# Norms by narrow matmuls of tokens and squares, with other matmul budgets per tick, in a hybrid scan, attention and experts kernel

## The chip, the cores and the metric

The kernel runs on one core of one Trainium2 chip. The metric is device time in microseconds (us) of one execution; the figure quoted for a kernel is the median of its runs. Besides the timed runs there is one profiled execution, from which all durations of single instructions come.

## The reference, cut to what matters

Four images of 384 channels and 32 x 32 places (1024 tokens) go through two layers. Layer 0 is a group norm, a selective scan in four directions with 16 states, a norm over channels, a GELU, and a residual sum. Layer 1 is a norm over channels, causal attention with one head of width 384, a residual sum, another norm over channels, and a mixture of 4 experts of which each token takes 2, with a residual sum.

```python
x = x + _L0_conv_ref(_gn(x), ...)          # scan; then norm over channels, GELU
t = _to_tokens(x)
t = t + _L1_attn_ref(_ln_t(t), Wq, Wk, Wv)
t = t + _L1_ffn_ref(_ln_t(t), gate_w, gate_b, w1, b1, w2, b2)

def _layernorm(x, axis=-1, eps=1e-5):
    m = jnp.mean(x, axis=axis, keepdims=True)
    v = jnp.var(x, axis=axis, keepdims=True)
    return (x - m) / jnp.sqrt(v + eps)
```

All of it is in float32. The norms that the change touches are the one after the scan (its result goes through the GELU) and the one ahead of the experts. The attention's own norm is another function and isn't edited.

## The kernel before, in words

**Layout.** Channels lie on the 128 partitions, three blocks of 128 (`M` = 3) beside each other; tokens lie along the free axis. A sum over channels is therefore a matmul with a matrix of 1/384 (`mean_w`).

**Ticks.** The kernel is one hand-written order, produced by a loop over ticks (the loop at the end of `hybrid_kernel`). There are 768 units of scan (4 images x 3 blocks x 4 directions x 4 groups of states x 4 groups of channels), one a tick; image b has ticks 192b to 192b + 191. In a tick, ScalarE makes the decay of the unit two ticks on (L554), VectorE makes the input product `v` (`front`, L561) and the scan (`middle`, L567), GpSimd multiplies the scan before by its output weights (`back`, L584), and each fourth tick TensorE sums four units into `y` (`row`, L609). In ticks 0 to 191 part of the products `v` is made on TensorE instead (`feed`, `turned`, L872). `ahead` makes VectorE wait, ahead of `v`, for the decay of its unit and, each fourth tick, for `y` of the four units before.

**Everything else is a generator that runs beside the scan.** A generator yields `("pe", n)` when it has issued matmuls that it declares at n us, `("wait", n)` to sleep n ticks, and `("inner", 0)` to go on in the next tick ahead of the scan rather than after it. In a tick the order is: decays, work that was deferred (`due`), `ahead`, `v`, `back`, deferred inner work, parked generators (`unpark`), the scan, `row`, fetches of the scan's operands (SP queue), one step of the preparation of a coming image (`preparation`, `project_dt`), and then `go_on`. `go_on` adds the pace to an allowance of TensorE time, lets every side generator issue until it has spent its own budget of 1.0 (it may overdraw), takes that from the allowance, and gives what is left to the first waiting generator, `behind(b)`: attention of image b, then its experts. The pace is `PACE_A` = 4.4 in attention and `PACE_E` = 3.3 otherwise. Side generators are `finish(b)` (block norm, GELU and residual of image b), `ready(b, h)` (expert norm and gates of half h), `fold` (once) and loads. After tick 767 there is no scan, and the loop goes on until all is issued.

**Image b after its scan.** `evict` (L629) adds the skip term to `y`; for the last block of channels it starts `finish(b)` and queues `behind(b)`. `behind` waits until `finish` has added the residual (L893), then runs `attention` and `experts`. Attention's scores use one folded matrix in place of Wq and Wk: `fold` centres and turns Wq and Wk (L746), multiplies them (L757) and centres Wv (L769), once, at tick 192, and stores both results to DRAM (`g_d`, `wv_d`); every image reads them from there.

**The norm before the change** (`layernorm(dst, src, name, lag)`, L636 to L712; `finish` calls it with 1024 tokens and lag 0, `ready` with 512 and lag 1):

1. For each half of 512 tokens, the mean over channels, on all 128 output partitions, by 3 full matmuls (L652); 2.6 is declared for each.
2. VectorE subtracts it from the tokens (L660).
3. ScalarE squares the result (L672).
4. Four matmuls side by side in four column groups of 32 give the variance of 128 tokens each, 12 for a half (L679).
5. ScalarE takes the root (L687), VectorE the reciprocal (L692).
6. TensorE spreads the reciprocals to all partitions (L698), and VectorE multiplies (L708).

**Shared buffers.** PSUM banks for all this are two before tick 192 and four after (`banks`); 8 tiles in SBUF are shared as `slots` (squares, `xr`, `dt`, `du`, expert weights, attention weights and so on). What is given back comes free a tick later for slots and at once for banks; a generator that finds none sleeps a tick. The buffers `a0` (1) and `ht` (2) are larger ones, used by fold, attention and experts.

Of the kernel before, what the change touches and what calls it, by code (L numbers as in the profile page):

```python
# [8 lines left out]
F32 = mybir.dt.float32  # L9
AF = mybir.ActivationFunctionType  # L10
ALU = mybir.AluOpType
# [4 lines left out]
P = 128  # L16
B = 4
C = 384
M = C // P
HW = 32  # L20
L = HW * HW
# [21 lines left out]
AHEAD = 5  # L43
SLOTS = 8
PACE_A = 4.4
PACE_E = 3.3


@with_exitstack
def hybrid_kernel(  # L50
# [22 lines left out]
    nc = tc.nc  # L73
# [4 lines left out]
    one = ctx.enter_context(tc.tile_pool(name="one", bufs=1))  # L78
# [34 lines left out]
    inner = {}  # L113
# [4 lines left out]
    class Shared:  # L118
# [520 lines left out]
    def layernorm(dst, src, name, lag):  # L639

        width = src.shape[2]
        n = width // 512
        mus = []
        for h in range(n):
            mu = yield from banks.take(f"mu_{name}_{h}")  # L650
            for c in range(M):
                nc.tensor.matmul(  # L652
                    mu, mean_w, src[:, c, bass.ts(h, 512)], start=(c == 0), stop=(c == M - 1)
                )
            mus.append(mu)
            yield "pe", 2.6
        yield "inner", 0
        for h in range(n):
            s = bass.ts(h, 512)
            nc.vector.tensor_tensor(  # L660
                dst[:, :, s], src[:, :, s], mus[h].unsqueeze(1).to_broadcast([P, M, 512]),
                ALU.subtract,
            )
            banks.give(f"mu_{name}_{h}")
        sqs = []
        for c in range(M):
            sq = yield from slots.take(f"sq_{name}_{c}", P, width)
# [22 lines left out]
        banks.give(f"var_{name}")  # L690
        yield "wait", 1
        nc.vector.reciprocal(rs, rs)  # L692
        yield "wait", lag
        backs = []
        for h in range(n):
            spread_ = yield from banks.take(f"rb_{name}_{h}")
            for q in range(4):
                nc.tensor.matmul(  # L698
                    spread_[:, q * P : (q + 1) * P],
                    ident[:, 32 * q : 32 * q + 1].to_broadcast([P, P]), rs[:, h, :],  # L700
                    start=True, stop=True,
                )
# [12 lines left out]

    def fold():

        extra = pools["a0"].tile([P, M, L], F32, tag="a0", name="w_extra")
        extra = extra.rearrange("p m l -> p (m l)")
        vs = extra[:, : 2 * M * C].rearrange("p (j c d) -> p j c d", j=2, c=M)
        centre = extra[:, 2 * M * C : 2 * M * C + 2 * P].rearrange("p (j d) -> p j d", j=2)
        nc.sync.dma_start(vs[:, 0], wv.rearrange("(c p) d -> p c d", p=P))
        for same in range(2):
            nc.vector.scalar_tensor_tensor(
                centre[:, same, :], ident, float(same), mean_w, ALU.mult, ALU.subtract
            )  # L730
        def square(name):
            t = pools["ht"].tile([P, M, L], F32, tag="ht", name=name)
            t = t.rearrange("p m l -> p (m l)")[:, : 2 * M * C]
            return t.rearrange("p (j c d) -> p j c d", j=2, c=M)

        raw = square("w_raw")
        for j, w in enumerate((wq, wk)):
            nc.sync.dma_start(raw[:, j], w.rearrange("(c p) d -> p c d", p=P))
        wt = square("w_t")
        yield "wait", 2  # L740
        for j in range(2):
            for d in range(M):
                ps = yield from banks.take(f"pwt_{j}_{d}")
                for c in range(M):
                    for o in range(M):
                        nc.tensor.matmul(  # L746
                            ps[:, c * P : (c + 1) * P], raw[:, j, o, d * P : (d + 1) * P],
                            centre[:, int(o == c), :], start=(o == 0), stop=(o == M - 1),
                        )
# [604 lines left out]
    def step(g, budget):  # L1354

        if g in ended:
            ended.remove(g)
            return None
        while budget > 0 and until.get(id(g), -100) <= clock[0]:
            try:  # L1360
                what, n = next(g)
            except StopIteration:
                return None
            if what == "pe":
                budget -= n
            elif what == "inner":
                parked.append(g)
                until[id(g)] = clock[0] + 1
            elif what == "start":
                started.append(1)  # L1370
                break
            elif n > 0:
                until[id(g)] = clock[0] + n
        return budget

    def go_on():
        spare[0] = min(spare[0] + pace[0], pace[0])
        for g in side[:]:
            left = step(g, 1.0)
            if left is None:  # L1380
                side.remove(g)
            else:
                spare[0] -= 1.0 - left
        while waiting and spare[0] > 0:
            left = step(waiting[0], spare[0])
            if left is None:
                waiting.pop(0)
                continue
            spare[0] = left
            break  # L1390
# [13 lines left out]
    t = 0  # L1404
# [86 lines left out]
```

## Time and profile before

| | |
|---|---|
| Median of 3 runs | 3749.89 us (3745.99 to 3752.34) |
| Profiled execution | 3747.14 us |
| Its span, first to last instruction | 3745.0 us |
| Busy: TensorE matmul | 3350.6 us (89%) |
| Busy: VectorE | 2961.6 us (79%) |
| Busy: ScalarE | 2085.8 us (56%) |
| Busy: GpSimd | 1817.8 us (49%) |
| Mean granted TensorE clock | 0.932 |

How to read the profile's lines. A group's line has the line of the kernel, the engine, the operation, what is written and read, and the size (partitions x elements). A wait's line has who waited, for whom, the sum in us, how often, and the longest. A line of the timeline has start, length, engine, line, operation and how many instructions were merged into it; in brackets is the idle time before it and what ended it. A line of a table by stretch has the stretch, its length, the busy time and number of instructions of TensorE, weight loads, VectorE, ScalarE and GpSimd, the granted clock, the busy share of DMA and GB/s. Each float32 matmul of the program is two records in the trace. A busy TensorE is not TensorE at its peak, since its records overlap.

### The profile page before, as it was taken

The numbers are of one execution on the slowest core, as the hardware profiler recorded it, in microseconds if no ns is written. First come the engines' busy times: TensorE is split into PE (matmuls) and PEld (weight loads), VectorE is DVE, ScalarE is ACT, GpSimd is POOL, SyncE is SP. The second block draws the span as 40 slices with busy tenths as digits, with TensorE's granted clock in tenths as the row PEclk, the third lists the DMA queues.
The fourth block names the chain that finished last, engine by engine and source line by source line (L and its number), as shares of the span: only waits on it lengthen the run. The fifth ranks groups of instructions, "written<-read, shape, count | busy, mean of one in ns | idle before, by whom it ended". The sixth has DMA issues, their size and how long they took to land. (4 is left out here: it accounts for less than half of the span.)

```text
span 3745.0 us, 35189 instructions
## 1 busy us (share of the span) xinstructions
PE 3350.6 (89%) x11891; PEld 1529.0 (41%) x11891; DVE 2961.6 (79%) x2084; ACT 2085.8 (56%) x2832; POOL 1817.8 (49%) x776
## 2 busy tenths in 40 slices
PE   4666667789999999898999999889999998999999
PEld 1333333345333343344333344454344444544444
DVE  5999899988998998989998999999999982210000
ACT  4788888556666555566655555455554552412121
POOL 2777777555565565545555665455665650000000
PEclk7677777899999999999999999899999999999999
DMA  6665666645665756436666665455657551322321
GB/s 204 219 233 199 208 218 221 215 145 199 235 222 201 260 206 230 155 138 228 217 221 229 201 210 192 146 182 188 223 192 240 179 182 38 92 82 83 96 82 53
DMA packets 408019, 680.03 MB, mean 182 GB/s; under 512 B 33520, under 2 KB 279968, under 8 KB 407840
## 3 DMA queue, kind: packets, MB, share of 16 engines
q1 hardware_dynamic: 401632, 677.40, 53.0%
q8 instruction: 94, 1.54, 0.2%
q10 hardware_dynamic: 6208, 0.39, 0.1%
q14 instruction: 85, 0.70, 0.1%
HBM read 605.16 MB, written 72.55 MB: 181 GB/s over the span
## 5 line engine op out<-in xcount | busy, mean ns | idle before, releaser
L584 POOL TENSOR_TENSOR h<-h,bc 128x1024 f32<-128x1024 f32 x768 | 1816.7, 2370 | 1264.9 <-DVE v L561 1058.3
L567 DVE TENSOR_TENSOR_SCAN h<-da,v 128x1024 f32<-128x1024 f32 x768 | 1748.4, 2283 | 48.4 <-PE v L872 17.3
L554 ACT ACTIVATE da<-dt,a 128x1024 f32<-128x1024 f32 x768 | 886.5, 1162 | 868.1 <-DVE h L567 759.3
L1297 PE MATMUL fy<-ht,w 128*128 128x512 f32 x2304 | 1019.8, 599 | 7.5 <-ACT ht L1261 5.9
L1272 PE MATMUL ph<-fx,w 128*128 128x512 f32 x2304 | 1019.1, 598 | 3.8 <-DMA w<-in_w 2.9
L561 DVE TENSOR_TENSOR v<-du,bc 128x1024 f32<-128x1024 f32 x664 | 842.8, 1269 | 61.9 <-DMA du<-dts 25.9
L1297 PEld LDWEIGHTS fy<-ht,w 128*128 128x128 f32 x2304 | 435.6, 191 | 580.3 <-issue 551.0
L1272 PEld LDWEIGHTS ph<-fx,w 128*128 128x128 f32 x2304 | 433.4, 191 | 579.6 <-issue 529.5
L609 PE MATMUL y<-h,sel 128*32 128x512 f32 x3072 | 493.3, 657 | 91.2 <-POOL h L584 89.2
L1257 ACT ACTIVATE ht<-ph,b1s 128x512 f32<-128x512 f32 x384 | 257.9, 679 | 471.0 <-PE ph L1272 469.2
L1306 DVE SCALAR_TENSOR_TENSOR fy<-fy,b2s,tw 128x512 f32<-128x512 f32 x96 | 72.0, 750 | 423.0 <-PE fy L1297 423.0
L609 PEld LDWEIGHTS y<-h,sel 128*32 128x32 f32 x3072 | 96.6, 115 | 399.3 <-issue 220.3
L850 ACT ACTIVATE st<-turn,bt 128x128 f32<-128x128 f32 x832 | 244.2, 554 | 0.0
L872 PE MATMUL v<-ident,st 128*128 128x128 f32 x832 | 147.5, 337 | 86.2 <-DVE h L567 85.4
L1261 ACT ACTIVATE ht<-ht 128x3072 f32<-128x3072 f32 x64 | 176.9, 2764 | 0.8
L872 PEld LDWEIGHTS v<-ident,st 128*128 128x128 f32 x832 | 121.7, 175 | 127.7 <-DVE h L567 74.2
L554 ACT ACT_TABLE_LOAD x99 | 127.0, 1283 | 18.7 <-DMA dt<-dts 12.3
L425 PE MATMUL pdt<-xd,wdt 12*128 12x512 f32 x184 | 88.0, 813 | 45.7 <-ACT dt L433 22.6
L1079 PE MATMUL po<-pt,vt 128*128 128x256 f32 x480 | 102.8, 364 | 7.1 <-ACT pt L971 7.1
L1009 PE MATMUL ss<-axn,qt 128*128 128x512 f32 (+3 forms) x288 | 102.3, 503 | 3.9 <-ACT yb L1096 3.9
L1079 PEld LDWEIGHTS po<-pt,vt 128*128 128x128 f32 x480 | 90.4, 192 | 22.3 <-ACT pt L971 10.1
L1009 PEld LDWEIGHTS ss<-axn,qt 128*128 128x128 f32 x288 | 51.5, 196 | 47.1 <-issue 33.5
(208 smaller groups left out, 1612.3 us busy)
## 6 DMA issues: line engine op xcount, KB each, us to landing
bc<-rows SPq DMA_DIRECT2D x384, 512.0 KB, 4.7
w<-in_w SPq DMA_DIRECT2D x384, 384.0 KB, 6.0
dt<-dts SPq DMA_DIRECT2D x192, 512.0 KB, 4.5
du<-dts SPq DMA_DIRECT2D x192, 512.0 KB, 6.6
dts<-dt SPq DMA_DIRECT2D x48, 512.0 KB, 4.7
dts<-du SPq DMA_DIRECT2D x48, 512.0 KB, 5.3
fx<-t2d SPq DMA_DIRECT2D x12, 768.0 KB, 5.5
tw<-mkd SPq DMA_DIRECT2D x32, 256.0 KB, 6.2
```

The source lines that it names most:

```text
L554: u["decay"] = nc.scalar.activation(u["da"], spread["dt4", n], AF.Exp, scale=a4[:, g, u["q"] : u["q"] + 1])
L561: return nc.vector.tensor_tensor(u["v"], spread["du4", n], spread["bc", n][:, 0, :], ALU.mult)
L567: nc.vector.tensor_tensor_scan(u["h"][:, ::step], u["da"][:, ::step], u["v"][:, ::step], 0.0, op0=ALU.mult, op1=ALU.add,)
L584: product = units[n]["product"] = nc.gpsimd.tensor_tensor(h, h, spread["bc", n][:, 1, :], ALU.mult)
L609: units[n]["row"] = nc.tensor.matmul(y, sel, h, start=first, stop=last, tile_position=(0, jj * DJ))
L850: nc.scalar.activation(st[:, 4 * h + t, :].rearrange("p (d i) -> p i d", i=NI)[:, i, :], ps[h][:, t * P : (t + 1) * P], AF.Copy, scale=bt[ ...
L872: nc.tensor.transpose(u["v"][:, t * P : (t + 1) * P], st[:, t, u["j"] * P : (u["j"] + 1) * P], ident)
L1079: nc.tensor.matmul(pv[:, o:], vt[:, j, m * P : (m + 1) * P], pts[step][j // 4][:, j % 4, o:], start=(alone and j == 0), stop=(j == nj - 1),)
L1257: nc.scalar.activation(ht[:, f, :], ps, AF.Identity, bias=bias)
L1261: nc.scalar.activation(ht, ht, AF.Gelu)
L1272: nc.tensor.matmul(ps, tiles[n][:, c, (f % 2) * P : (f % 2 + 1) * P], xns[h][:, c, :], start=(c == 0), stop=(c == M - 1),)
L1297: nc.tensor.matmul(pss[m], tiles[n][:, f, :], hts[fh][:, f, :], start=(fh == 0 and f == 0), stop=(fh == 1 and f == FH - 1),)
```

## The change

- `layernorm` no longer subtracts first. It squares the tokens themselves, takes the means of tokens and of squares by matmuls in four column groups (12 each for a half), makes the variance as mean of squares less squared mean, and forms 1/root and mean/root on 128 x 256 elements (or 128 x 128). TensorE spreads both, and VectorE multiplies the tokens by the one and subtracts the other. The results are kept in the first tile of squares, no longer in a tile of their own. It declares 0.7 for each 12 matmuls of means and 1.8 for each half's spreading.
- Side generators may issue until they have spent `BESIDE` = 3.0 a tick instead of 1.0. `PACE_E` goes from 3.3 to 3.2.
- `fold` issues two banks' work a tick instead of one. Its Wv and its centring matrices move from the `a0` buffer to three slots, and it stores both results at the end.
- For image 0, `attention` makes the normed tokens before it waits for `fold` and loads the folded weights; for the other images the order stays.

```diff
@@ -43,7 +43,8 @@
 AHEAD = 5
 SLOTS = 8
 PACE_A = 4.4
-PACE_E = 3.3
+PACE_E = 3.2
+BESIDE = 3.0
 @with_exitstack
@@ -645,23 +646,6 @@
         width = src.shape[2]
         n = width // 512
-        mus = []
-        for h in range(n):
-            mu = yield from banks.take(f"mu_{name}_{h}")
-            for c in range(M):
-                nc.tensor.matmul(
-                    mu, mean_w, src[:, c, bass.ts(h, 512)], start=(c == 0), stop=(c == M - 1)
-                )
-            mus.append(mu)
-            yield "pe", 2.6
-        yield "inner", 0
-        for h in range(n):
-            s = bass.ts(h, 512)
-            nc.vector.tensor_tensor(
-                dst[:, :, s], src[:, :, s], mus[h].unsqueeze(1).to_broadcast([P, M, 512]),
-                ALU.subtract,
-            )
-            banks.give(f"mu_{name}_{h}")
         sqs = []
         for c in range(M):
             sq = yield from slots.take(f"sq_{name}_{c}", P, width)
@@ -669,47 +653,54 @@
         for h in range(n):
             for c in range(M):
                 s = bass.ts(h, 512)
-                nc.scalar.activation(sqs[c][:, s], dst[:, c, s], AF.Square)
+                nc.scalar.activation(sqs[c][:, s], src[:, c, s], AF.Square)
         yield "wait", lag
+
         var = yield from banks.take(f"var_{name}")
-        for h in range(n):
-            for c in range(M):
-                for q in range(4):
-                    o = h * 512 + q * P
-                    nc.tensor.matmul(
-                        var[32 * q : 32 * (q + 1), h * P : (h + 1) * P], mean_w[:, :32],
-                        sqs[c][:, o : o + P], start=(c == 0), stop=(c == M - 1),
-                        tile_position=(0, 32 * q),
-                    )
-            yield "pe", 1.0
-        slots.give(*[f"sq_{name}_{c}" for c in range(M)])
-        rs = one.tile([P, n, P], F32, tag=f"rs{n}", name=f"rs_{name}")
-        nc.scalar.activation(
-            rs, var[:, : n * P].rearrange("p (h t) -> p h t", t=P), AF.Sqrt, bias=eps
-        )
+        w = n * P
+        for o, of in ((w, [src[:, c, :] for c in range(M)]), (0, sqs)):
+            for h in range(n):
+                for c in range(M):
+                    for q in range(4):
+                        k = h * 512 + q * P
+                        nc.tensor.matmul(
+                            var[32 * q : 32 * (q + 1), o + h * P : o + (h + 1) * P],
+                            mean_w[:, :32], of[c][:, k : k + P],
+                            start=(c == 0), stop=(c == M - 1), tile_position=(0, 32 * q),
+                        )
+                yield "pe", 0.7
+        slots.give(*[f"sq_{name}_{c}" for c in range(1, M)])
+        rs = sqs[0][:, :w]
+        mean = sqs[0][:, w : 2 * w]
+        nc.scalar.activation(rs, var[:, w : 2 * w], AF.Square)
+        yield "inner", 0
+        nc.vector.tensor_tensor(rs, var[:, :w], rs, ALU.subtract)
+        nc.scalar.activation(rs, rs, AF.Sqrt, bias=eps)
+        yield "wait", 1
+        nc.vector.reciprocal(rs, rs)
+        nc.vector.tensor_tensor(mean, var[:, w : 2 * w], rs, ALU.mult)
         banks.give(f"var_{name}")
-        yield "wait", 1
-        nc.vector.reciprocal(rs, rs)
         yield "wait", lag
-        backs = []
-        for h in range(n):
-            spread_ = yield from banks.take(f"rb_{name}_{h}")
-            for q in range(4):
-                nc.tensor.matmul(
-                    spread_[:, q * P : (q + 1) * P],
-                    ident[:, 32 * q : 32 * q + 1].to_broadcast([P, P]), rs[:, h, :],
-                    start=True, stop=True,
-                )
-            backs.append(spread_)
-            yield "pe", 1.0
-        yield "inner", 0
         for h in range(n):
             s = bass.ts(h, 512)
-            nc.vector.tensor_tensor(
-                dst[:, :, s], dst[:, :, s], backs[h].unsqueeze(1).to_broadcast([P, M, 512]),
-                ALU.mult,
-            )
-            banks.give(f"rb_{name}_{h}")
+            while not banks.ready(2):
+                yield "wait", 1
+            both = [banks.now(f"{x}_{name}_{h}") for x in ("rb", "mb")]
+            for x, v in zip(both, (rs, mean)):
+                for q in range(4):
+                    nc.tensor.matmul(
+                        x[:, q * P : (q + 1) * P],
+                        ident[:, 32 * q : 32 * q + 1].to_broadcast([P, P]),
+                        v[:, h * P : (h + 1) * P], start=True, stop=True,
+                    )
+            yield "pe", 1.8
+            if h == n - 1:
+                slots.give(f"sq_{name}_0")
+            yield "inner", 0
+            x, y = (v.unsqueeze(1).to_broadcast([P, M, 512]) for v in both)
+            nc.vector.tensor_tensor(dst[:, :, s], src[:, :, s], x, ALU.mult)
+            nc.vector.tensor_tensor(dst[:, :, s], dst[:, :, s], y, ALU.subtract)
+            banks.give(*[f"{x}_{name}_{h}" for x in ("rb", "mb")])
     folded = []
@@ -719,62 +710,74 @@
-        extra = pools["a0"].tile([P, M, L], F32, tag="a0", name="w_extra")
-        extra = extra.rearrange("p m l -> p (m l)")
-        vs = extra[:, : 2 * M * C].rearrange("p (j c d) -> p j c d", j=2, c=M)
-        centre = extra[:, 2 * M * C : 2 * M * C + 2 * P].rearrange("p (j d) -> p j d", j=2)
-        nc.sync.dma_start(vs[:, 0], wv.rearrange("(c p) d -> p c d", p=P))
+        def square(name):
+            t = pools["ht"].tile([P, M, L], F32, tag="ht", name=name)
+            t = t.rearrange("p m l -> p (m l)")[:, : 2 * M * C]
+            return t.rearrange("p (j c d) -> p j c d", j=2, c=M)
+
+        raw = square("w_raw")
+        for j, w in enumerate((wq, wk)):
+            nc.sync.dma_start(raw[:, j], w.rearrange("(c p) d -> p c d", p=P))
+        va = yield from slots.take("va", P, 2, C)
+        vb = yield from slots.take("vb", P, C)
+        centre = yield from slots.take("centre", P, 2, P)
+        wvs = wv.rearrange("(c p) d -> p c d", p=P)
+        nc.sync.dma_start(va, wvs[:, :2, :])
+        nc.sync.dma_start(vb, wvs[:, 2, :])
+        vs = (va[:, 0, :], va[:, 1, :], vb)
         for same in range(2):
             nc.vector.scalar_tensor_tensor(
                 centre[:, same, :], ident, float(same), mean_w, ALU.mult, ALU.subtract
             )
-        def square(name):
-            t = pools["ht"].tile([P, M, L], F32, tag="ht", name=name)
-            t = t.rearrange("p m l -> p (m l)")[:, : 2 * M * C]
-            return t.rearrange("p (j c d) -> p j c d", j=2, c=M)
-
-        raw = square("w_raw")
-        for j, w in enumerate((wq, wk)):
-            nc.sync.dma_start(raw[:, j], w.rearrange("(c p) d -> p c d", p=P))
         wt = square("w_t")
-        yield "wait", 2
-        for j in range(2):
-            for d in range(M):
-                ps = yield from banks.take(f"pwt_{j}_{d}")
-                for c in range(M):
-                    for o in range(M):
-                        nc.tensor.matmul(
-                            ps[:, c * P : (c + 1) * P], raw[:, j, o, d * P : (d + 1) * P],
-                            centre[:, int(o == c), :], start=(o == 0), stop=(o == M - 1),
-                        )
-                yield "wait", 1
-                nc.scalar.copy(wt[:, j, d, :], ps[:, :C])
-                banks.give(f"pwt_{j}_{d}")
-        g = square("g_s")[:, 0]
-        for m in range(M):
-            ps = yield from banks.take(f"pg_{m}")
+
+        def turned_weight(j, d, ps):
+            for c in range(M):
+                for o in range(M):
+                    nc.tensor.matmul(
+                        ps[:, c * P : (c + 1) * P], raw[:, j, o, d * P : (d + 1) * P],
+                        centre[:, int(o == c), :], start=(o == 0), stop=(o == M - 1),
+                    )
+            return lambda: nc.scalar.copy(wt[:, j, d, :], ps[:, :C])
+
+        def product(m, ps):
             for d in range(M):
                 nc.tensor.matmul(
                     ps[:, :C], wt[:, 0, d, m * P : (m + 1) * P], wt[:, 1, d, :],
                     start=(d == 0), stop=(d == M - 1),
                 )
-            yield "wait", 1
-            nc.scalar.activation(g[:, m, :], ps[:, :C], AF.Copy, scale=-scale)
-            banks.give(f"pg_{m}")
-        yield "wait", 1
-        nc.sync.dma_start(g_d, g)
-        for m in range(M):
-            ps = yield from banks.take(f"pwv_{m}")
+            return lambda: nc.scalar.activation(both[:, 0, m, :], ps[:, :C], AF.Copy, scale=-scale)
+
+        def centred(m, ps):
             for c in range(M):
                 nc.tensor.matmul(
-                    ps[:, :C], centre[:, int(c == m), :], vs[:, 0, c, :],
+                    ps[:, :C], centre[:, int(c == m), :], vs[c],
                     start=(c == 0), stop=(c == M - 1),
                 )
-            yield "wait", 1
-            nc.scalar.copy(vs[:, 1, m, :], ps[:, :C])
-            banks.give(f"pwv_{m}")
-        yield "wait", 1
-        nc.sync.dma_start(wv_d, vs[:, 1])
+            return lambda: nc.scalar.copy(both[:, 1, m, :], ps[:, :C])
+
+        def by_twos(what, jobs):
+            for n in range(0, len(jobs), 2):
+                some = jobs[n : n + 2]
+                while not banks.ready(len(some)):
+                    yield "wait", 1
+                names = [f"{what}_{n + i}" for i in range(len(some))]
+                moves = [f(banks.now(name)) for f, name in zip(some, names)]
+                yield "wait", 1
+                for move in moves:
+                    move()
+                banks.give(*names)
+
+        yield "wait", 2
+        pairs = [(j, d) for d in range(M) for j in range(2)]
+        yield from by_twos("pwt", [lambda ps, j=j, d=d: turned_weight(j, d, ps) for j, d in pairs])
+        both = square("g_s")
+        jobs = [lambda ps, m=m: product(m, ps) for m in range(M)]
+        yield from by_twos("pg", jobs + [lambda ps, m=m: centred(m, ps) for m in range(M)])
+        slots.give("va", "vb", "centre")
+        nc.sync.dma_start(g_d, both[:, 0])
+        nc.sync.dma_start(wv_d, both[:, 1])
+        yield "wait", 1
         folded.append(1)
@@ -954,8 +957,10 @@
     def attention(b, yb, fx0):
         alone = b == B - 1
-        while not folded:
-            yield "wait", 1
+        if b == 0:
+            xn = yield from scaled_tokens(b, yb)
+            while not folded:
+                yield "wait", 1
         gw_ = []
         for name, w in ((f"wg_{b}", g_d), (f"wv_{b}", wv_d)):
             ta = yield from slots.take(f"{name}a", P, 2, C)
@@ -963,7 +968,8 @@
             tb = yield from slots.take(f"{name}b", P, C)
             nc.sync.dma_start(tb, w[:, 2, :])
             gw_.append((ta[:, 0, :], ta[:, 1, :], tb))
-        xn = yield from scaled_tokens(b, yb)
+        if b > 0:
+            xn = yield from scaled_tokens(b, yb)
         qt = pools["ht"].tile([P, M, L], F32, tag="ht", name=f"qt_{b}")
         vt = pools["ht"].tile([P, L // P, C], F32, tag="ht", name=f"vt_{b}")
@@ -1376,11 +1382,11 @@
     def go_on():
         spare[0] = min(spare[0] + pace[0], pace[0])
         for g in side[:]:
-            left = step(g, 1.0)
+            left = step(g, BESIDE)
             if left is None:
                 side.remove(g)
             else:
-                spare[0] -= 1.0 - left
+                spare[0] -= BESIDE - left
         while waiting and spare[0] > 0:
             left = step(waiting[0], spare[0])
             if left is None:
```

More of the change, by code (lines that the diff above doesn't have):

```diff
@@ L685, in layernorm @@
-        slots.give(*[f"sq_{name}_{c}" for c in range(M)])
-        rs = one.tile([P, n, P], F32, tag=f"rs{n}", name=f"rs_{name}")
-        nc.scalar.activation(
-            rs, var[:, : n * P].rearrange("p (h t) -> p h t", t=P), AF.Sqrt, bias=eps
-        )
-        banks.give(f"var_{name}")
+        w = n * P
[10 more added lines that the diff above has]
+                yield "pe", 0.7
@@ L691, in layernorm @@
+        slots.give(*[f"sq_{name}_{c}" for c in range(1, M)])
[5 more added lines that the diff above has]
+        nc.scalar.activation(rs, rs, AF.Sqrt, bias=eps)
         yield "wait", 1
         nc.vector.reciprocal(rs, rs)
+        nc.vector.tensor_tensor(mean, var[:, w : 2 * w], rs, ALU.mult)
+        banks.give(f"var_{name}")
@@ L723, in fold @@
-        extra = extra.rearrange("p m l -> p (m l)")
-        vs = extra[:, : 2 * M * C].rearrange("p (j c d) -> p j c d", j=2, c=M)
-        centre = extra[:, 2 * M * C : 2 * M * C + 2 * P].rearrange("p (j d) -> p j d", j=2)
-        nc.sync.dma_start(vs[:, 0], wv.rearrange("(c p) d -> p c d", p=P))
-        for same in range(2):
-            nc.vector.scalar_tensor_tensor(
-                centre[:, same, :], ident, float(same), mean_w, ALU.mult, ALU.subtract
-            )
         def square(name):
@@ L738, in fold @@
             nc.sync.dma_start(raw[:, j], w.rearrange("(c p) d -> p c d", p=P))
-        wt = square("w_t")
-        yield "wait", 2
-        for j in range(2):
-            for d in range(M):
-                ps = yield from banks.take(f"pwt_{j}_{d}")
-                for c in range(M):
-                    for o in range(M):
-                        nc.tensor.matmul(
-                            ps[:, c * P : (c + 1) * P], raw[:, j, o, d * P : (d + 1) * P],
-                            centre[:, int(o == c), :], start=(o == 0), stop=(o == M - 1),
-                        )
-                yield "wait", 1
-                nc.scalar.copy(wt[:, j, d, :], ps[:, :C])
-                banks.give(f"pwt_{j}_{d}")
-        g = square("g_s")[:, 0]
-        for m in range(M):
-            ps = yield from banks.take(f"pg_{m}")
+        va = yield from slots.take("va", P, 2, C)
[5 more added lines that the diff above has]
+        vs = (va[:, 0, :], va[:, 1, :], vb)
+        for same in range(2):
+            nc.vector.scalar_tensor_tensor(
+                centre[:, same, :], ident, float(same), mean_w, ALU.mult, ALU.subtract
+            )
+        wt = square("w_t")
+        def turned_weight(j, d, ps):
[4 more added lines that the diff above has]
+                        centre[:, int(o == c), :], start=(o == 0), stop=(o == M - 1),
+                    )
+            return lambda: nc.scalar.copy(wt[:, j, d, :], ps[:, :C])
+        def product(m, ps):
             for d in range(M):
```

## The prediction

> **What bounds the kernel now.** I read the page's engine shares first, then busy time by stretch, then VectorE's waits, then the order of time on single engines. The page's slices show two regimes: VectorE 80 to 99% busy up to the last scan, TensorE alone after it. By stretch (time, engines' busy time, clock, DMA):
>
> ```profile
> 675.00:3083.00 2408.00, 2281.06 (x8033) 1007.53 (x8032) 2282.62 (x1581) 1395.19 (x1486) 1361.04 (x577) 0.97 0.59 201
> 3083.00:3145.00 62.00, 49.29 (x273) 25.97 (x272) 22.81 (x19) 17.19 (x19) 0.33 (x1) 0.89 0.17 58
> 3145.00:3745.00 600.00, 590.73 (x1588) 282.20 (x1587) 65.11 (x131) 148.05 (x189) 0.00 (x0) 1.00 0.26 76
> ```
>
> The columns after the span are PE, weight loads, VectorE, ScalarE, GpSimd. From 675 (scan 192, where the change begins to act) to 3083 (the last scan is over) TensorE and VectorE are both busy for 2281 and 2283 us of 2408. Which one leads? In a stretch of pure experts:
>
> ```profile
> 2621.00:3083.00 462.00, 459.69 (x1397) 185.14 (x1396) 450.33 (x277) 254.47 (x241) 285.14 (x121) 1.00 0.61 206
> ```
>
> VectorE is at 97.5% there with gaps of tens of ns, so it leads; TensorE's 99% is generous, since its records overlap. Its need per tick is 3.3 us of experts (PACE_E) plus 16 records of `y` in some 1.9 us each fourth tick, 3.3 + 0.5 = 3.8; VectorE's is scan 2.28 + `v` 1.26 + 0.2 for the experts' output, and the tick measures 3.85. They are nearly level, so TensorE's lag reaches VectorE where something extra comes. What VectorE waited for in 675 to 3083:
>
> ```profile
> DVE nb L1026 <- PE ss L1014: 17.0, 7, 9.5
> DVE du L441 <- PE fy L1297: 15.2, 6, 6.7
> DVE v L561 <- PE y L609: 11.1, 9, 3.7
> DVE du L441 <- PE ph L1272: 10.6, 3, 8.9
> DVE du L441 <- ACT dt L433: 5.1, 3, 2.6
> ```
>
> The old norms hardly stand in that list (sums of 1.4 to 1.8 us): each matmul of theirs has two ticks until VectorE wants it. Last, TensorE between the last scan and the last image's attention:
>
> ```profile
> 3109.56 5.42 PE L1297 MATMUL fy<-ht,w 128*128 128x512 f32 x12
> 3114.82 1.05 PE L698 MATMUL rb_l<-rs_l,ident 128*128 128x128 f32 x8
> 3115.71 5.32 PE L1297 MATMUL fy<-ht,w 128*128 128x512 f32 x12
> 3120.86 1.05 PE L698 MATMUL rb_l<-rs_l,ident 128*128 128x128 f32 x8
> 3127.63 0.66 PE L914 MATMUL var_at<-yb,mean_w 128*32 128x128 f32 x8 [5.71 <-DVE yb L893]
> 3128.76 0.65 PE L914 MATMUL var_at<-yb,mean_w 128*32 128x128 f32 x8 [0.48 <-DVE yb L893]
> 3131.29 1.94 PE L914 MATMUL var_at<-yb,mean_w 128*32 128x128 f32 x32 [1.87 <-DVE yb L893]
> ```
>
> Image 2's experts end in the tail (72 `fy` records from 3080 on, 31 us), under image 3's norm; then TensorE waits 5.7 + 0.5 + 1.9 = 8.1 us for the tokens. After that it is TensorE alone.
>
> **What the skill says.** "TensorE: Matmul & The Clock Gate", Part 3: matmuls into different groups of 32 columns run at the same time. The trace agrees: 48 records of `var_l` took 1.52 us (32 ns each), while 8 of `rb_l`, the same width but full, took 1.05 (131 ns). Same page, "Architectural detail": VectorE and ScalarE queues are strictly first in, first out. It agrees: scan 298 stood 6.03 us behind a `du`. "ScalarE: Activation LUTs", "What ACT_TABLE_LOAD costs": 1283 ns plus a drain of some 1380; the page's mean is 1283, but a load of 1.28 us at 1128.87 is followed by its activation at 1130.17, so I use 1.3.
>
> **The change, part by part.** A call on fp32 leaves two records (1152 calls of `fy`, 2304 records), and 12 records 512 wide take 5.15 us in the tail: 0.43 each.
>
> *TensorE's work.* Block norm now: mu 5.31 + var 1.52 + rb 2.10 = 8.9 us. New: 96 var records in 3.0 and 32 of rb and mb in 4.2: 7.2, less by 1.7. Expert norm, half as wide: 4.4 to 3.7, less by 0.7, twice an image. So 3.1 us an image: 9.4 over images 0 to 2, 3.1 in the tail.
>
> *VectorE's work.* The wide subtract and multiply stay (1.74 us a half). New: one narrow subtract and one narrow multiply; the 128x256 subtract of L925 takes 0.42, half that width some 0.25. 0.84 + 2 x 0.5 = 1.8 us an image, three images before the last scan: **+5.6**, with nothing to hide it.
>
> *Shorter notice.* Block norm: squares and all var matmuls go out in the evict's own tick, and the next tick begins with VectorE's subtract. Squares take 3.3 us from the evict (six at 0.55), the last matmuls 0.5, the new square 0.4, hand-overs 0.3: 4.5, against scan + `v` of 3.55. That is 1 us late, and more behind a gelu (2.8 plus loads). Expert norm: var (1.6) + square (0.3) + 0.2 = 2.1 after a scan, against 1.3 for the next `v`: 0.8 late plus TensorE's lag. Today's mu begins -1.7 to +2.0 us, mean 0.7, after the scan of its tick. Later rb has one tick instead of two: 0.7 + lag against 1.3, mostly covered. What stands behind the waiting VectorE instruction is the scan, and behind that GpSimd's product, `y`, everything. A wait can't gain; if every cover holds it costs 0, with lag up to 5 us twice a norm some 35 in all. By the middle: 3 x 2.5 + 6 x 1.7 = 18, less a third because a stop lets TensorE catch up (a lag is paid once): **+12**.
>
> *Image 0's start.* The tick map (scans counted; ScalarE's decays mark its order) has evict 0 in tick 195, tokens finished 206, fold done 208, first `pq` 211. New norm: var 195, subtract 196, reciprocal and rb 197, halves 198 and 199, adds 200 and 201. The fold's twelve banks go by twos: six steps from 194, done 201. But it now holds three of eight slots until then, and the three `xr` need slots too: tokens at about 203, `pq` near 206.5, 4.5 ticks sooner. Moved with it: `wg`/`wv` loads now follow the norm, directly ahead of `pq`, on the SP queue behind the scan's fetches. `wg_0a` took 5.6 us to land; TensorE stands that long and ScalarE's copies with it; two ticks of slack cover part: **+3** (0 to 8).
>
> *Pace.* An image's experts declare 8 x (12 x 2.6 + 6 x 5.1) = 494.4 us: 149.8 ticks at 3.3, 154.5 at 3.2, +4.7. The norms declare 9.2 to 6.4 and 4.6 to 3.2 twice: -5.6, or 1.7 ticks less, of which I count 1.3. So +3.4 ticks an image. Today experts end at 397, 589 and about 779.5, and tokens 1 and 2 are ready at 398 and 590, five ticks sooner from now on. Image 1 then starts at 397 (-1), image 2 at 592 (+2), image 2's experts end at 784.5 (+5). Work left at the last scan grows by 5 x 3.2 - 1 = 15 us.
>
> *Relief.* 15 + 9 us less TensorE work before the last scan only helps where VectorE waits for TensorE, some 60 us of the list and its smaller rows. The `du` waits are a matter of phase (a slot still read by an expert's matmul, bursts of 5.1), so lower load removes a part only: **-12** (bounds 0 and -25).
>
> *Tail.* +15 of experts, -8.1 of waiting (tokens are ready by 3125, experts end near 3130, so the chain is covered; without that cover it comes back), -3.1 of norms: **+4**. What is late next is the attention norm's chain, 3136 to 3144, unchanged.
>
> *By-twos weights, BESIDE for gates, stage one:* nothing. Before tick 192 nothing else declares TensorE time, and the fold's matmuls are the same 36 x 3 and 18 + 18 records, with TensorE 72 to 82% busy there.
>
> **Sum.** 5.6 + 12 + 3 - 12 + 4 = +12.6 us. The profiled execution took 3747.1 us (span 3745.0), 2.8 below the median of 3749.9; from the median: **3762**, slower by 0.3%. A measurement of this kernel tells about 0.2% (7.5 us) from no change.
>
> **Rivals.**
> 1. *TensorE leads* (faster). It speaks for it that every long VectorE wait names TensorE and that it is at 1.00 in most stretches of ticks 240 to 380. Then each us taken from it before the last scan is a us gained, up to the 60 of waits: -24, tail +4, the new waits vanish in the lag they replace: 3730. It decides once TensorE's lag at the norms is over some 2 us all the time. Against it: 97.5% VectorE in ticks 648 to 768, and a mean lag of 0.7.
> 2. *One tick is too short everywhere* (slower still). The norm's two waits meet lags of 4 to 5 us, as the attention's `nb` did (up to 9.5): 35 instead of 12, 3785. Slots add to it if image 0 starts no sooner.
>
> **Chances.** Forecast 0.55 (0.14 of it within 0.2%, 0.41 slower), rival 1 0.28 (faster), rival 2 0.17 (slower). Faster 0.28, same 0.14, slower 0.58. The range 3725 to 3795 takes in both rivals and the bounds of waits and relief; under 3725 is 0.09, above 3795 0.08.
>
> **What would show it.** Right: new VectorE waits at the narrow subtract, 1 to 3 us each; first `pq` some 4 ticks sooner; 45 us of `fy` after the last scan instead of 31; no 8 us gap before `var_at` of image 3. The forecast is wrong if VectorE's gaps (83 us over 0.3 us each in 675 to 3083) fall by over 20, or if the norm's subtracts never wait.

## The result, and the profile after

The changed kernel takes 3802.12 us in the median (3796.4 to 3805.4, four runs) against 3750.35 before: a ratio of 1.0135, with a 95% interval of 1.0123 to 1.0148. It is 52 us slower; 3762 was forecast, with 3795 as the upper end. The profiled execution has a span of 3801.6 us, against 3745.0.

By stretch, from scan 192 to the last scan, from there to the last image's first `pq`, and to the end:

```profile
682.00:3131.00 2449.00, 2287.76 (x8320) 1020.26 (x8321) 2288.56 (x1598) 1388.49 (x1488) 1355.42 (x576) 0.96 0.58 197
3131.00:3192.20 61.20, 53.96 (x346) 28.94 (x344) 22.78 (x21) 20.43 (x24) 2.94 (x2) 0.97 0.22 72
3192.20:3801.60 609.40, 597.84 (x1643) 289.07 (x1642) 67.78 (x136) 148.70 (x191) 0.00 (x0) 0.98 0.25 75
```

The reader is to see that the loss lies in the first line: 2449 us against 2408 for the same 576 scans, while VectorE's busy time grew by 6 only. Cut exactly at the ends of scans 191 and 767, the stretch is 2452.1 against 2406.9, 45.2 more. The remainder is 5.8 us behind the last scan (counted to the last arithmetic instruction) and 5.4 ahead of scan 192. In the latter stretch the four compute engines run the same instructions in the same order in both kernels and in all of e1 to e11 below; those eleven stand at -1.3 to +2.6 us against before, so I take the 5.4 as the scatter of one execution.

What VectorE waited for between scan 192 and the last scan:

```profile
DVE v L562 <- PE y L610: 24.4, 7, 6.3
DVE sq_ff L677 <- ACT sq_ff L675: 18.5, 3, 12.5
DVE nb L1032 <- PE ss L1020: 15.2, 8, 5.5
DVE du L442 <- PE ph L1278: 8.7, 2, 8.3
DVE v L562 <- ACT da L555: 7.8, 2, 5.2
DVE fx L701 <- PE rb_ff L691: 6.0, 4, 3.5
DVE sq_l L677 <- ACT sq_l L675: 5.8, 3, 3.5
```

The old names are still there (`nb`, `du`, `v`); new are the narrow subtract (L677) and the wide multiply (L701) of the norm. The longest wait, 12.5 us, stands in image 0, at the norm of its second half of tokens. The orders of VectorE and then of TensorE around it:

```profile
911.00 2.29 DVE L568 TENSOR_TENSOR_SCAN h<-da,v 128x1024 f32<-128x1024 f32 x1
918.47 1.23 DVE L562 TENSOR_TENSOR v<-du,bc 128x1024 f32<-128x1024 f32 x1 [5.18 <-ACT da L555]
919.74 2.29 DVE L568 TENSOR_TENSOR_SCAN h<-da,v 128x1024 f32<-128x1024 f32 x1
924.66 1.23 DVE L562 TENSOR_TENSOR v<-du,bc 128x1024 f32<-128x1024 f32 x1 [2.64 <-ACT da L555]
938.41 0.29 DVE L677 TENSOR_TENSOR sq_ff<-var_ff,sq_ff 128x128 f32<-128x128 f32 x1 [12.51 <-ACT sq_ff L675]
938.62 2.28 DVE L568 TENSOR_TENSOR_SCAN h<-da,v 128x1024 f32<-128x1024 f32 x1
```

```profile
905.79 0.28 PE L1175 MATMUL pm<-ident,mk 128*16 128x128 f32 x1
911.78 4.67 PE L1278 MATMUL ph<-fx,w 128*128 128x512 f32 x6 [5.71 <-DMA w<-in_w]
916.28 2.74 PE L393 MATMUL pxd<-x,wx 128*128 128x512 f32 x6
918.86 2.74 PE L1278 MATMUL ph<-fx,w 128*128 128x512 f32 x6
921.43 2.74 PE L393 MATMUL pxd<-x,wx 128*128 128x512 f32 x6
924.01 7.89 PE L1278 MATMUL ph<-fx,w 128*128 128x512 f32 x18
931.83 1.92 PE L610 MATMUL y<-h,sel 128*32 128x512 f32 x16
933.68 2.84 PE L393 MATMUL pxd<-x,wx 128*128 128x512 f32 x6
936.45 0.86 PE L666 MATMUL var_ff<-fx,mean_w 128*32 128x128 f32 x24
937.13 0.84 PE L666 MATMUL var_ff<-sq_ff,mean_w 128*32 128x128 f32 x24
```

An instruction of 0.29 us held the scans for 12.5, because its matmuls stood at the end of TensorE's queue: behind 5.7 us in which the experts' first weights hadn't landed, the experts' first matmuls and the next image's projections. One tick of notice can't bridge such a backlog.

Last, TensorE between the last scan and the last image's attention:

```profile
3148.22 5.42 PE L1303 MATMUL fy<-ht,w 128*128 128x512 f32 x12
3155.11 1.16 PE L691 MATMUL rb_l<-sq_l,ident 128*128 128x128 f32 x8 [1.48 <-DVE sq_l L680]
3156.11 1.06 PE L691 MATMUL mb_l<-sq_l,ident 128*128 128x128 f32 x8
3158.12 1.16 PE L691 MATMUL rb_l<-sq_l,ident 128*128 128x128 f32 x8 [0.95 <-DVE yb L701]
3159.97 1.16 PE L691 MATMUL mb_l<-sq_l,ident 128*128 128x128 f32 x8 [0.70 <-DVE yb L702]
3160.97 20.77 PE L1303 MATMUL fy<-ht,w 128*128 128x512 f32 x48
3181.66 1.52 PE L917 MATMUL var_at<-yb,mean_w 128*32 128x128 f32 x48
```

Here the step went as it was put: the experts' matmuls now outlast the norm, and `var_at` follows without the wait of 5.7 us.

### The profile page after: what moved, and what is told of

It is laid out like the page before. It is cut to its first block, busy times and chain, and to the rows that moved or that the text cites. A ratio compares the mean times of both kernels' runs of the same rounds, so it can differ in the third digit from the quotient of the medians.

```text
span 3801.6 us, 36066 instructions
## 1 busy us (share of the span) xinstructions
PE 3369.8 (89%) x12307; PEld 1551.9 (41%) x12307; DVE 2971.0 (78%) x2108; ACT 2082.8 (55%) x2842; POOL 1815.8 (48%) x776
## 4 chain that ended last, share of the span: by engine, by line
PE 43%; DVE 39%; ACT 8%; issue 5%; DMA 4%; POOL 1%; SPq 1%; DVEq 0%; ACTq 0%; POOLq 0%
DVE h L568 22%; PE ph L1278 14%; PE fy L1303 13%; DVE v L562 12%; PE y L610 4%; ACT da L555 2%; PE po L1085 2%; ACT st L853 2%; PE pq L986 2%; PE pv L997 2%; DMA du<-dts 2%; PE ss L1015 1%; PE pxd L393 1%; PE pdt L426 1%; PE v L875 1%
## 5 line engine op out<-in xcount | busy, mean ns | idle before, releaser
L562 DVE TENSOR_TENSOR v<-du,bc 128x1024 f32<-128x1024 f32 x664 | 840.2, 1265 | 72.7 <-PE y L610 24.4
L610 PE MATMUL y<-h,sel 128*32 128x512 f32 x3072 | 508.1, 658 | 101.2 <-POOL h L585 99.2
L1085 PE MATMUL po<-pt,vt 128*128 128x256 f32 x480 | 115.7, 397 | 18.8 <-ACT pt L977 18.8
L1085 PEld LDWEIGHTS po<-pt,vt 128*128 128x128 f32 x480 | 99.7, 213 | 38.8 <-ACT pt L977 23.3
L434 ACT ACTIVATE dt<-pdt,dtb 128x512 f32<-128x512 f32 x92 | 58.2, 683 | 20.2 <-PE pdt L426 19.8
```

What stands on the lines that cost most here:

```text
L562: return nc.vector.tensor_tensor(u["v"], spread["du4", n], spread["bc", n][:, 0, :], ALU.mult)
L610: units[n]["row"] = nc.tensor.matmul(y, sel, h, start=first, stop=last, tile_position=(0, jj * DJ))
L1085: nc.tensor.matmul(pv[:, o:], vt[:, j, m * P : (m + 1) * P], pts[step][j // 4][:, j % 4, o:], start=(alone and j == 0), stop=(j == nj - 1),)
```

## The experiments

All ratios are against the kernel before, on the same chip, with 95% intervals. For every run I also took figures from its trace, so that a run tells more than its time: the length of the stretch from scan 192 to the last scan; the idle time of VectorE in it (gaps over 0.3 us), split into gaps ahead of an instruction of `layernorm` and all others; the experts' matmul records left between the last scan and the last image's first `pq` (0.43 us each); and the time from the last scan to the last arithmetic instruction.

| Kernel | Ratio | Scan 192 to last, us | Gaps at the norm | Other gaps | Records left | Behind the last scan |
|---|---|---|---|---|---|---|
| before | 1 | 2406.9 | 3.2 | 80.3 | 70 | 659.9 |
| changed | 1.0135 | 2452.1 | 39.3 | 80.5 | 87 | 665.7 |
| e1, changed, old norm | 1.0123 | 2435.2 | 48.3 | 62.0 | 102 | 679.5 |
| e2, before, new norm | 1.0010 | 2423.5 | 5.0 | 87.0 | 42 | 649.3 |
| e3, changed, a tick more | 1.0040 | 2423.9 | 8.3 | 84.0 | 102 | 661.5 |
| e4, changed, weights first | 1.0132 | 2432.2 | 21.3 | 79.6 | 126 | 690.9 |
| e5, changed, budget 1.0 | 1.0042 | 2420.8 | 9.0 | 79.1 | 102 | 664.6 |
| e6, before, pace 3.2 | 1.0066 | 2395.2 | 3.0 | 71.9 | 167 | 696.7 |
| e7, changed, old fold | 1.0130 | 2443.9 | 28.8 | 83.6 | 108 | 674.2 |
| e8, before, budget 3.0 | 1.0063 | 2434.5 | 33.2 | 75.5 | 46 | 655.6 |
| e9, e2, later projections | 1.0008 | 2420.4 | 3.6 | 87.1 | 42 | 649.4 |
| e10, changed, later projections | 1.0100 | 2436.0 | 26.2 | 78.9 | 93 | 668.4 |
| e11, before, later projections | 0.9979 | 2396.7 | 1.6 | 70.7 | 70 | 659.9 |

The first theory was that of the prediction: the new norm's structure gives VectorE too short a notice. The rival put it down to the other parts: budget, pace, fold.

**e1, the old norm in the changed kernel.** `layernorm` is that of before, line for line.

> The changed kernel with the norm of before; budgets, fold and attention order stay changed. Theory 1 (the new norm's shorter notice makes VectorE wait, about 39 us of gaps stand at its narrow subtracts and its multiplies): some 30 of the 52 us go, about 3770. Theory 2 (the budgets and the new order of fold and attention cost the time, the norm is a bystander): at most 10 us go, about 3795.

3796.15 us, 1.0123 (1.0108 to 1.0138). The first theory fails as it stood. Yet the gaps at the norm didn't go: they are 48 us, now at the old norm's wide subtract and multiply:

```profile
DVE v L562 <- PE y L610: 22.3, 9, 6.6
DVE fx L661 <- PE mu_ff L653: 22.2, 6, 10.9
DVE nb L1042 <- PE ss L1030: 12.6, 7, 4.6
DVE fx L709 <- PE rb_ff L699: 10.6, 5, 3.5
DVE yb L709 <- PE rb_l L699: 9.3, 3, 7.1
```

So the waits belong to something that both norms meet in the changed kernel.

**e2, the new norm alone.** The kernel before with the new `layernorm`; budget 1.0, pace 3.3, old fold.

> The kernel before with the new norm alone; budget 1.0, pace 3.3 and the old fold stay. Theory 1: slower by some 30 us, about 3780. Theory 2: within 10 us of before, about 3755.

3754.11 us, 1.0010 (1.0003 to 1.0016). Its gaps are 5.0 us, as small as before. With a budget of 1.0 the norm stops after two yields of 0.7, and after the first of 1.8, and what follows comes a tick later; with 3.0 it goes on within the tick. The tick of notice is put in by the budget.

**e3, one more tick in the changed kernel.**

```diff
         nc.scalar.activation(rs, var[:, w : 2 * w], AF.Square)
+        yield "wait", 1
         yield "inner", 0
...
                 slots.give(f"sq_{name}_0")
+            yield "wait", 1
             yield "inner", 0
```

> The changed kernel with one more tick between the norm's matmuls and the VectorE instruction that reads them, at both places; no other edit. Theory 1: gaps at the narrow subtract and at the wide multiply nearly vanish, 25 to 35 us go, about 3772. Theory 2: no more than 8 us go, since the image's end comes two to three ticks later in exchange, about 3798.

3766.23 us, 1.0040 (1.0025 to 1.0055): 36 us go, and the gaps at the norm fall from 39.3 to 8.3. The narrow subtract that had waited 12.5 us waits 4.1:

```profile
925.39 0.29 DVE L678 TENSOR_TENSOR sq_ff<-var_ff,sq_ff 128x128 f32<-128x128 f32 x1 [4.06 <-ACT sq_ff L675]
```

**e4, the experts' first weights two ticks ahead.**

```diff
         load(0)
+        yield from need(0)
+        yield "wait", 2
```

> The changed kernel with the experts' first weights requested two ticks ahead of their first matmul. The trace shows TensorE standing 5.7 us for them in image 0, with ScalarE's decays, an `y` and the narrow subtract of the second half behind it (23 us of VectorE gaps in ticks 239 to 242). If this wait is what makes those gaps: 12 to 20 us go, about 3787. If the backlog of the attention does it anyway: under 5 us, about 3800.

3800.07 us, 1.0132 (1.0115 to 1.0149). The time says that nothing was gained; the table says otherwise. The stretch of scans is 20 us shorter and the norm's gaps fall to 21, but the two ticks an image leave 126 records behind the last scan instead of 87, and 25 us more there. The gap of 12.5 us is 0.8 here. So the wait for weights did feed it, and this remedy pays it back in the tail.

The third theory, from e1 to e3: the budget of 3.0 is the cost, since it lets the norm's matmuls and the VectorE instruction that reads them follow each other within a tick, whichever norm it is. Its rival: pace or fold.

**e5, budget back to 1.0 in the changed kernel** (`BESIDE = 1.0`).

> The changed kernel with the side budget put back to 1.0; the new norm, pace 3.2 and the new fold stay. Theory 3 (the larger budget is the cost: it lets the norm's matmuls and the VectorE instruction that reads them follow within one tick, whichever norm it is): 30 to 40 us of the 52 go, about 3766. Theory 4 (pace 3.2 or the new fold cost the time): no more than 10 us go, about 3795.

3764.69 us, 1.0042 (1.0027 to 1.0057): 37 us go, gaps at the norm 9.0.

**e6, pace 3.2 in the kernel before** (`PACE_E = 3.2`).

> The kernel before with pace 3.2 alone. Theory 3: the experts end about 4.7 ticks an image later, 14 in all, of which the slack takes little, so 15 to 30 us of matmuls move behind the last scan and part of it comes back in front: about 3760. Theory 4 with the pace as the cause: 3785 or more.

3773.76 us, 1.0066 (1.0049 to 1.0083), slower than I expected of it. 97 records more are left (42 us of matmuls), and the time behind the last scan grows by 37; ahead of it the scans gain 12 us. So 42 us of TensorE work less are worth about a quarter there, and some 2 of the 12 us are VectorE's own work for the same experts.

**e7, the old fold and the old order of image 0's attention in the changed kernel.** `fold` and the head of `attention` are those of before.

> The changed kernel with the old fold and the old order in attention of image 0. Theory 3: image 0 starts later by some 4 ticks, and the loss in ticks 192 to 207 (15 us) stays, since the norm makes it: 3800 to 3812. Theory 4 with the fold as the cause: the 15 us of ticks 192 to 207 go, about 3785.

3797.31 us, 1.0130 (1.0115 to 1.0145). In ticks 192 to 207 the changed kernel's loss of 15 us (from +5.4 to +20.1 against before) is gone: -1.0. So in that place the fold takes part, against my expectation, but only together with the budget of 3.0 and the short notice: e5 (new fold, budget 1.0), e8 (old fold, 3.0) and e3 (both, with the added tick) end it at -2.0, +0.6 and -0.1, while e1, with both and the old norm, loses 14. Some 6 of the changed kernel's 15 us come back by tick 220 anyway, and in the sum the old fold gains little: the stretch of scans is 8 us shorter than in the changed kernel, the time behind it 8.5 us longer.

**e8, budget 3.0 in the kernel before.**

```diff
-            left = step(g, 1.0)
+            left = step(g, BESIDE)
...
-                spare[0] -= 1.0 - left
+                spare[0] -= BESIDE - left
```

> The kernel before with the side budget 3.0 alone. Theory 3: VectorE waits appear at the wide subtract and the wide multiply of the old norm (in the changed kernel with the old norm these were 22 + 11 + 9 + 7 us), about 3780. Theory 4: no change, about 3751.

3772.61 us, 1.0063 (1.0048 to 1.0078). The budget alone turns 3.2 us of gaps at the norm into 33.2, in the unchanged norm. The subtract of the second half's mean in image 0, before and here:

```profile
918.06 1.75 DVE L660 TENSOR_TENSOR fx<-fx,mu_ff 128x1536 f32<-128x1536 f32 x1 [1.37 <-PE mu_ff L652]
```

```profile
915.37 1.54 DVE L562 TENSOR_TENSOR v<-du,bc 128x1024 f32<-128x1024 f32 x1
925.91 1.75 DVE L661 TENSOR_TENSOR fx<-fx,mu_ff 128x1536 f32<-128x1536 f32 x1 [9.00 <-PE mu_ff L653]
```

With a budget of 1.0 the mean's 2.6 end the tick, and the subtract has two ticks. That settles what makes the gaps at the norm: e3, e5 and e8 move them by 30 us each, in both directions and in both norms. How much of the 52 us it is, is weighed below.

**e9 to e11, the next image's projections later.** In e2, one VectorE wait of 14.0 us stands at tick 249, where the projections meet the start of the experts. One edit in three kernels:

```diff
-        while clock[0] < IMAGE * (b - 1) + 24:
+        while clock[0] < IMAGE * (b - 1) + 60:
```

> The kernel before with the new norm alone, and the preparation of the next image held to tick 60 of an image instead of 24, so that its projections no longer fall on the start of the experts (in the run with the new norm alone one VectorE wait of 14.0 us stands there, at tick 249). If that wait is a collision of the two: 10 to 17 us go against 3754, so about 3740, faster than before. If the preparation only carries its waits along: 3750 to 3756.

3752.09 us, 1.0008 (0.9999 to 1.0016): a miss. The wait at tick 249 is gone (+20.0 us at tick 255 against before became +0.5), but others came later (9.2 us at tick 347, 7.9 at 451), and the last scan is only 3 us earlier.

> The changed kernel with the preparation held to tick 60. If the start of the experts meets the projections in the 23 us of gaps of ticks 239 to 242: 10 to 20 us go, about 3787; the norm's gaps elsewhere (some 25 us) stay. If the budget alone makes them: under 5 us, about 3800.

3787.46 us, 1.0100 (1.0086 to 1.0114): 15 us go; the gaps at the norm are 13 us smaller, the rest of them stays, as expected.

> The kernel before with the preparation held to tick 60, as a control. Its own gaps in ticks 242 to 248 are 9 us; if these are the same collision, 5 to 9 us go, about 3742; if not, no change, 3750.

3740.71 us, 0.9979 (0.997 to 0.9988): faster than both kernels, by 0.2% against before. Its sum of gaps is 72 us instead of 83.5.

## Why the prediction was wrong, point by point

The difference of the spans is 56.6 us. In the prediction's own terms:

| Step | Put at | Measured |
|---|---|---|
| VectorE's work | +5.6 | +7.3 (sum of durations from scan 192 to the last scan) |
| Shorter notice | +12 | +36 (gaps at the norm 3.2 to 39.3) |
| Image 0's start | +3 | 0: the first `pq` followed its tokens with no wait for `wg_0` |
| Relief | -12 | 0 (other gaps 80.3 to 80.5) |
| Tail | +4 | +5.8 |
| Ahead of scan 192 | 0 | +5.4, scatter |
| Gaps under 0.3 us | not in the sum | +1.1 |

- **The step that failed is "Shorter notice".** Its mechanism was right, that the narrow subtract and the multiply wait with the scan behind them; its size was off by three, 36 us instead of 12. I took TensorE's lag from the mean of today's `mu` starts (0.7 us), but in image 0 the matmuls of the second half are issued as the experts begin, where TensorE is far behind: this one norm's three waits are 12.5 + 1.0 + 3.7 us. A wait is set by the backlog at its own place, not by a mean over the kernel. The other eight norms have 22 us together, near the 16 that my 2.5 and 1.7 a norm make for them. And the third that I took off, because a stop would let TensorE catch up, didn't come back. Rival 2 came nearest, with 35 us, but by luck: nine norms with two waits of up to 5 us could make up to 90, and one tick wasn't "too short everywhere", since nearly half of the gaps stand at one norm.
- **I also put the notice down to the wrong part.** The prediction describes it as the new norm's order. e2 and e8 show that it is the budget: the new norm with 1.0 has 5 us of gaps, the old one with 3.0 has 33. The prediction put `BESIDE` at "nothing", with a reason that holds before tick 192 only; that all `var` matmuls go out in one tick, which it counts on, is this budget's doing (four yields of 0.7 fit into 3.0 and not into 1.0).
- **"Relief" failed too.** It was sized at half of the TensorE work removed. e6 measured a better price: 42 us less TensorE work took 8.4 us of other gaps and shortened the stretch by 12. The changed kernel left only 17 records (7.3 us) more behind the last scan, so that there was less to relieve than the 24 us I used: 9.4 of norms and 7.3 of experts. A quarter of 17 would be 4; not even that shows. But the 0 is a net: behind `fy`, the waits of `du` fell from 15.2 to 2.7 us, those of `v` for `y` rose from 11.1 to 24.4, and new ones came (5.0 behind the GELU, 5.2 and 2.6 ahead of the 12.5), so that some relief may be hidden in it.
- **Tail: right in sum, by other terms, which is luck.** The records left rose by 17, not 35. With the budget at 1.0 (e5) they rose by 32, so the tick counts were about right; the budget, put at nothing, takes 15 of them off again (24 in e8 against before). The first `pq` came 61.0 us after the last scan (63.1 before). But from there to the last instruction it took 604.7 us instead of 596.8: see the last section.
- **The tick map held.** Subtract in tick 196, halves in 198 and 199, tokens of image 0 finished in 203, `pq` in tick 207 (forecast near 206.5, 211 before). The residual's first add met one gap that I hadn't priced, 5.0 us behind the GELU.
- **Rival 1 (TensorE leads) is refuted by e6**: if each microsecond of TensorE work counted, the scans would have gained 42 us and not 12.

**How the loss divides.** Step by step from before: the new norm (e2) +0.10%, then pace 3.2 and the new fold (e5 against e2) +0.32%, then the budget +0.93%; with the intervals of the runs, each step is known to 0.1 to 0.2 points. The second step moves 60 records behind the last scan and makes the time there 15.3 us longer, for 2.7 us gained ahead of it. Each part alone in the kernel before makes another division: norm 0.10%, pace 0.66%, budget 0.63%, the fold alone not tried. So the budget is worth about a half to two thirds of the loss. The pace is a second cause: with the fold it has a quarter in the first division, by itself nearly a half in the second. The norm itself costs little.

In other figures, e5 has all but the budget and is about 16 us slower than before (0.42%). Against before it has 5.8 us of gaps more at the norm, 8.7 us more VectorE work and 4.7 us more behind the last scan, which together with -1.3 ahead of scan 192 and -1 of other gaps is 17. What stays open is how the second step divides between pace and fold; pace 3.3 in the changed kernel wasn't tried. The new norm alone (e2) gains 10.6 us behind the last scan and gives 16.6 back ahead of it: 28 records fewer are left, so the scans carry 12 us more of experts, beside 7 us of VectorE's own work.

## What to carry to other kernels

Where instructions of several engines are put into one hand-written order, the distance between a producer's issue and its consumer's place in a strictly ordered queue is a resource; a budget that looks like a limit on work may be what supplies it. Before such a limit is raised, list each consumer that stands in the bound engine's queue and compare its notice with the producer's worst backlog at that place, not with the mean. And a gain ahead of the end should be looked for together with what is left for the end: e2, e4 and e6 moved work between the two with hardly any change, or a loss, in the sum.

## What the runs showed of the hardware that was not expected

The tail's attention was slower for the same matmuls. In the changed kernel TensorE stood 2.4 us ahead of a `po` and then 2.1 us ahead of `pgate`, within 15 us; in e5 the second stop is missing. Stretches over the same work (changed, then e5); the number after the five busy times is TensorE's granted clock:

```profile
3261.00:3293.00 32.00, 29.84 (x140) 26.36 (x141) 9.49 (x23) 5.65 (x10) 0.00 (x0) 0.79 0.28 87
```

```profile
3229.00:3262.00 33.00, 31.51 (x155) 25.28 (x156) 9.06 (x19) 8.25 (x14) 0.00 (x0) 0.95 0.42 132
```

0.79 against 0.95. Cut finer, the changed kernel's stretch is at half clock around the end of the first stop (3261.1) and again just after the second (3276.2):

```profile
3260.60:3267.20 6.60, 6.09 (x15) 4.97 (x16) 1.25 (x2) 2.41 (x4) 0.00 (x0) 0.50 0.01 2
3267.40:3277.40 10.00, 7.95 (x56) 7.28 (x55) 4.62 (x4) 0.97 (x2) 0.00 (x0) 1.00 0.41 117
3277.70:3284.30 6.60, 6.60 (x26) 5.92 (x27) 0.62 (x4) 2.67 (x4) 0.00 (x0) 0.50 0.66 222
```

Between the first `pq` and the end, the `po` matmuls took 28.1 us against 24.0 before and 25.5 in e5, and `pgate` 6.5 against 5.2; TensorE's idle time there differs by 1.9 us only (5.3 against 3.4). So most of the 7.9 us came as slower matmuls near two short stops, not as the stops themselves.

All thirteen kernels fall into two groups. The six with budget 3.0 and no added tick (changed, e1, e4, e7, e8, e10) have a second stop ahead of `pgate`, of 1.1 to 2.1 us, a clock of 0.79 to 0.84 over the 32 us from the end of the first stop, and 604 to 607 us from the first `pq` on. The other seven, e3 with the same budget and an added tick among them, have no such stop, 0.95 to 1.00, and 597 to 599 us. That the stops make the clock fall is suggested by this, and not shown: no run changed a stop alone. Nor does every stop do it: the first stop before, of 2.2 us, had no half clock after it (1.00 over the next 32 us).
